# A quarter of the scan steps woven into the attention of the last image, and a sigmoid written as a tanh

## The chip, the core and the metric

The kernel runs on one core of a Trainium2 chip. The core has five engines that run beside each other, each through its own instructions in order: PE (TensorE, matrix products), DVE (VectorE), ACT (ScalarE, activation functions and copies), POOL (GpSimd) and SP (which here only issues DMAs). All data are float32. The metric is the time of one execution in microseconds on the device: 3661.46 us, the median of three runs (3655.79 to 3663.48).

## The reference

Four images of 64 x 64 pixels (L = 4096 tokens) with 128 channels go through four layers one after another:

- layer 0: neighbourhood attention with 7 x 7 windows and a gate, added to x
- layer 1: group norm, then attention of all 4096 tokens to all 4096, added to x
- layer 2: `out = (x W_left + x W_eq) * sum over a row of (x W_right) * sigmoid(x W_gate)`, projected, added to x, layer norm
- layer 3: projection to 512 channels, a 3 x 3 depthwise convolution and SiLU on half of them, then four selective scans, a gate, a norm and an output projection

The scan is what the change is about:

```python
dt_kb = dt.reshape(K, Bb, r, L)              # dt comes as [image, direction]
delta = softplus(delta + dbias); du = delta * u
def step(xc, inp):                           # along the 4096 tokens
    xc = exp(dlt * A) * xc + dut * Bt
    y = xc * Ct
```

The reshapes exchange images and directions in part of the operands: a scan with indices (k, b) takes its delta from image b, and its u, B and C from image k; b and k together say in which of four orders (forward, reversed, transposed, transposed and reversed) they are read. There are 4 k, 4 b and 2 halves f of the 256 channels, so 32 scans of 4096 tokens, 128 channels each. The scans with k and b in {0, 1} need images 0 and 1 only, and no transposed order.

## The kernel before

**Order of the work.** `layers_0_to_2` goes through the images one by one. For each it runs layer 0, then `layer_1`, and woven into `layer_1`'s loop, by the function `between` that is called every eight steps, layer 2 of the same image (`turn`, `mix`, `add`, `norm` by chunks of 512 tokens) and the front of layer 3 (`front`: projection, convolution, SiLU, and the small projection to delta's rank, B and C) of half of the image before and half of this one. What the front makes goes to DRAM: `ub_d` (u times B), `dbl_d` (ten rows: eight for delta, B and C), `ct_d` (C transposed), `zf_d` (the gate) and `y_d` (the sum of the y, which starts as D times u). An odd image adds its part with an accumulating DMA from POOL (line 982), and `copy_du` (line 950) copies that sum to the other three targets. `layer_3` then runs all scans and the output.

A scheduler at compile time orders each engine's instructions by priority (the order of the program) and by its own estimate of when operands are ready; `tc.keep_in_program_order` pins an instruction in its place, and `tc.issue_after(ins)` puts what is traced inside it behind `ins` on that engine.

**`layer_1`** has 16 blocks of 256 queries and 16 groups of 256 keys per block, 279 steps with the run-out. A step multiplies two score tiles (line 636), ACT copies them to SBUF (`st`, 640), DVE keeps a running maximum (`mx`, 642). When a block is complete its maxima are turned (650, 652), spread by a product with ones (`dm`, `pb`, 655 and 659), DVE adds them to the scores (662) and ACT takes the Exp (663), in four pieces of 2048. The values of the block follow 23 steps behind the scores (`po`, 672). PSUM has eight banks: four slots "s" (scores and nearly all 512-column products), two "t", two "o" (`po`). SBUF has five "ring" buffers of 16 KB per partition; in `layer_1` they hold x, the normed x and three rings of scores.

**The end of the last image.** `end(i)` runs the last chunks (4 to 7) of image 3's front, from i = 30 to 40. `diagonals` (line 905, 18 small POOL products) makes the weights with which PE does part of the convolution (`convolve_by_pe`, 918) at i = 35 to 38. At i = 32 the first loads of layer 3 are issued: `early.dbl` (rows of images 0 and 1), `early.ub` and `early.cb` (1085 to 1088).

**`layer_3`** has a list `todo` of 64 pairs of steps of 1024 tokens (128 steps), four k times four parts (f and a pair of b) times four places. A pair takes: two twice-512-column products with eight rows (`pdt`, line 1268), Softplus on ACT (`de`, 1275), `inp = de * ub` on POOL (1279), Exp on ACT into PSUM (`h`, 1292), the scan on DVE (1306), the last column kept (`end`, 1309), the product with C on DVE (`yo`, 1320), and an accumulating DMA from POOL to `y_d` (1321). `load_ub` (1214) and `load_c` (1218) bring u times B and C, four or eight pairs ahead. The k = 0 pairs with b = 0, 1 come first.

Of the kernel before, what the change touches and what calls it, by code (L numbers as in the profile page):

```python
# [29 lines left out]
P = 128  # L30
# [4 lines left out]
CH = 512  # L35
# [46 lines left out]
def conv_seq(ctx, tc, x, mata, matb, cols, rows, rpb, dtw, convw, sel, out):  # L82
# [51 lines left out]
    layers_0_to_2(tc, xf, mata, matb, rows, rpb, convw, sel, ident, cl, dram, big, ring, early, *fronts)  # L134
# [4 lines left out]
def layers_0_to_2(  # L139
    ctx, tc, xf, mata, matb, rows, rpb, convw, sel, ident, cl, dram, big, ring, early, x3_d, ub_d, zf_d, y_d, dbl_d, ct_d, gw_d, bw_d  # L140
# [110 lines left out]
    nc.vector.tensor_scalar(b_rs, cl("b_right"), float(W), None, ALU.mult)  # L251

# [322 lines left out]
    def layer_1(b, xt, hT, st, between):  # L575
# [55 lines left out]
        def score(i, k, g):  # L631
            if g == 0:
                k.mx = tmp.tile([P, G, QB], F32, name="mx1", tag="mx1")
            ps = ps_s([P, G, QB], "sc1")
            for r in range(G):
                nc.tensor.matmul(  # L636
                    ps[:, r, :], lhsT=kT[:, bass.ts(G * g + r, P)], rhs=qT[:, bass.ts(i, QB)], start=True, stop=True
                )
            st = group(ng * i + g)
            nc.scalar.copy(st, ps)  # L640
            if g > 0:
                nc.vector.tensor_tensor(k.mx, group(ng * i) if g == 1 else k.mx, ps, ALU.max)  # L642
# [4 lines left out]
        def turn_maxima(k):  # L647
            pt = ps_t([P, 2, P], "pt1")
            for h in range(2):
                nc.tensor.transpose(pt[:, h, :], k.mx[:, 0, bass.ts(h, P)], ident)  # L650
            nm = sml.tile([P, 2], F32, name="nm1", tag="nm1")
            nc.vector.tensor_reduce(nm, pt, AX.X, ALU.max, negate=True)
            k.dm = tmp.tile([P, 2, P], F32, name="dm1", tag="dm1", bufs=1)
            for h in range(2):
                nc.vector.tensor_scalar(k.dm[:, h, :], ident, nm[:, h:h + 1], None, ALU.mult)

        def soften(i, k):
            pb = ps_t([P, QB], "pb1")
            nc.tensor.matmul(pb, lhsT=ones, rhs=k.dm.rearrange("p h q -> p (h q)"), start=True, stop=True)  # L659
# [22 lines left out]

        blocks = {}
        for s in range(ng * (NB + 1) + LAG):
# [11 lines left out]
            if j >= 0:  # L696
                value(j, blocks[j], gv)
                if gv == ng - 1:
                    finish(j, blocks.pop(j))
            t = s // 8  # L700
# [14 lines left out]
    def layer_2(b, xt):  # L715
# [9 lines left out]
        def mix(n):  # L725
# [4 lines left out]
            nc.vector.tensor_scalar(rt, pr, b_rs, None, ALU.add)  # L730
# [3 lines left out]
            nc.scalar.activation(sg, pg, AF.Sigmoid, bias=cl("b_gate"))  # L734
# [3 lines left out]
            nc.vector.scalar_tensor_tensor(o1, pl, b_le, sg, ALU.add, ALU.mult)  # L738
# [54 lines left out]
    def front(b):  # L793
# [248 lines left out]
        def end(i):  # L1042
# [37 lines left out]
            if i == NT:  # L1080
# [7 lines left out]
                nc.sync.dma_start(early.cb, dbl_d[0][RANK + 1:RANK + 2, :][0].partition_broadcast(P))  # L1088

        def turn(i):  # L1090
# [41 lines left out]
            if b == B - 1 and i == 6:  # L1132
# [4 lines left out]
        return turn  # L1137

# [5 lines left out]
    for b in range(B):  # L1144
# [25 lines left out]
        layer_1(b, xt, *handed.pop(b), between)  # L1170
# [10 lines left out]
def layer_3(ctx, tc, of, dt, na, ident, cl, big, early, x3_d, ub_d, zf_d, y_d, dbl_d, ct_d, gw_d, bw_d):  # L1181
# [34 lines left out]
    def load_c(k, t):  # L1216

        nc.sync.dma_start(cb_s[t], bc_d[k][1 + t][0].partition_broadcast(P))
# [19 lines left out]
    with pool("s", 2) as sp, pool("psC", 2, space=PSUM) as psp:  # L1238
# [5 lines left out]
        for k in range(B):  # L1244
            one, two = k & 1, 1 - (k & 1)
            for part, f in enumerate((one, two, two, one)):
                loads = []
                if part == 0:
                    loads = [(load_ub, two, k), (load_c, k, 1)]
                elif part == 2 and k + 1 < B:  # L1250
                    loads = [(load_c, k + 1, 0)]
                elif part == 3 and k + 1 < B:
                    loads = [(load_ub, two, k + 1)]
                for at_n in range(NSC):
                    n = NSC - 1 - at_n if k & 1 else at_n
                    todo.append((loads, [(f, k, 2 * (part >> 1) + q, n) for q in range(2)]))
# [40 lines left out]
        def back(f, k, b, n, inp, h):  # L1297
# [12 lines left out]
            cb = cb_s[b >> 1]  # L1310
# [247 lines left out]
```

## Time and profile before

| | us |
|---|---|
| median of the runs | 3661.46 |
| profiled execution | 3660.97 |
| its span | 3659.2 |
| PE busy | 3296.5 (90%) |
| DVE busy | 2777.9 (76%) |
| ACT busy | 2645.6 (72%) |
| POOL busy | 1418.6 (39%) |
| layer 1 of the last image, first score to last value | 2413.7 to 2960 |
| scans | 3020 to 3492 |
| output | 3492 to 3659 |

Times inside the span count from its start. In the profile's lists a row has start, duration, engine, line, operation, written tile and read tiles, shapes, count, and in brackets the idle time before it and what ended that. PEld is PE's loading of weights, which runs beside its products. A matmul of float32 has two records. Shares of busy time are means over a window; in the rows by window the numbers behind the five engines are the granted TensorE clock (1 is full), the mean busy share of the 16 DMA engines, and GB/s.

### The profile page before, as it was taken

How to read it: one execution, taken by the hardware profiler on the slowest of the kernel's cores; microseconds unless marked ns; L12 is line 12 of the kernel's file. 1: busy time of each engine (PE TensorE's matmuls, PEld its weight loads, DVE VectorE, ACT ScalarE, POOL GpSimd, SP SyncE). 2: the span in 40 equal slices, each digit the busy share in tenths (PEclk: the TensorE clock that was granted, in tenths of full speed). 3: DMA queues.
4: the chain of work that ended last, by engine and by line, in shares of the span. 5: the costliest groups of instructions: out<-in, count | busy, mean ns of one | idle time of the engine just before them, and what ended most of it. 6: DMA issues, size and time to landing. Idle time of an engine off the chain costs nothing. (4 is left out here: it accounts for less than half of the span.)

```text
span 3659.2 us, 61463 instructions
## 1 busy us (share of the span) xinstructions
PE 3296.5 (90%) x22234; PEld 2603.3 (71%) x22234; DVE 2777.9 (76%) x5069; ACT 2645.6 (72%) x4325; POOL 1418.6 (39%) x1592
## 2 busy tenths in 40 slices
PE   7999999999999999998999999989999987666647
PEld 4679988866788888666888886668888852222236
DVE  5767777767767787676787776767877758999968
ACT  4855667778677777786777777867777769999934
POOL 6500012245112222451122223521222338999856
PEclk8999999999999999999999999999999995555579
DMA  4200000131001012410021213100101279999998
GB/s 125 71 25 3 12 18 27 54 101 34 24 30 41 28 47 86 134 37 24 24 79 30 76 54 101 40 1 24 45 30 36 67 219 217 214 237 218 202 275 282
DMA packets 189362, 310.38 MB, mean 85 GB/s; under 512 B 23007, under 2 KB 111996, under 8 KB 184156
## 3 DMA queue, kind: packets, MB, share of 16 engines
q1 hardware_dynamic: 146260, 220.27, 18.0%
q0 software_dynamic: 24384, 76.95, 11.8%
q10 hardware_dynamic: 18416, 9.24, 0.9%
q8 instruction: 176, 2.88, 0.3%
q14 instruction: 126, 1.03, 0.1%
HBM read 167.69 MB, written 155.56 MB: 88 GB/s over the span
## 5 line engine op out<-in xcount | busy, mean ns | idle before, releaser
L672 PEld LDWEIGHTS po<-v,st 128*128 128x128 f32 x8192 | 1049.1, 193 | 73.6 <-issue 35.7
L672 PE MATMUL po<-v,st 128*128 128x129 f32 x8192 | 1067.9, 277 | 17.6 <-ACT st L663 17.6
L636 PE MATMUL sc<-qT,kT 128*128 128x256 f32 x4096 | 1025.8, 382 | 13.3 <-DVE mx L642 13.1
L640 ACT COPY st<-sc 128x512 f32<-128x512 f32 x1024 | 582.4, 585 | 465.8 <-PE sc L636 463.0
L642 DVE TENSOR_TENSOR mx<-mx,sc 128x512 f32<-128x512 f32 x896 | 613.3, 684 | 283.7 <-ACT st L640 259.4
L636 PEld LDWEIGHTS sc<-qT,kT 128*128 128x128 f32 x4096 | 719.4, 191 | 105.9 <-issue 17.7
L662 DVE TENSOR_TENSOR st<-st,pb 128x2048 f32<-128x2048 f32 x256 | 572.5, 2280 | 29.0 <-PE pb L659 28.7
L663 ACT ACTIVATE st<-st 128x2048 f32<-128x2048 f32 x256 | 484.8, 1911 | 28.8 <-DVE st L662 27.5
L1268 PE MATMUL pdt<-dbl,dt 8*128 8x512 f32 x512 | 307.6, 1081 | 142.1 <-ACT de L1275 141.4
L1279 POOL TENSOR_TENSOR inp<-de,ub 128x1024 f32<-128x1024 f32 x128 | 409.9, 4405 | 9.7 <-ACT de L1275 8.2
L1268 PEld LDWEIGHTS pdt<-dbl,dt 8*128 8x128 f32 x512 | 114.1, 312 | 332.7 <-ACT de L1275 269.8
L503 POOL TENSOR_SCALAR pr<-pr,sm 128x308 f32<-128x308 f32 (+3 forms) x512 | 244.7, 497 | 204.6 <-DVE sm L501 187.6
L743 POOL TENSOR_TENSOR x<-x,row 128x512 f32<-128x512 f32 x32 | 47.9, 1496 | 706.3 <-DVE mx L642 687.6
L889 POOL TENSOR_TENSOR gsum<-gsum,tp 128x504 f32<-128x504 f32 (+1 forms) x177 | 229.7, 1303 | 131.3 <-ACT gsum L877 77.3
L495 ACT ACTIVATE pr<-pr,mx 128x308 f32<-128x308 f32 (+3 forms) x512 | 263.0, 518 | 1.4 <-DVE mx L484 1.4
L1306 DVE TENSOR_TENSOR_SCAN h<-h,end,inp 128x1024 f32<-128x1024 f32 x96 | 221.1, 2346 | 20.0 <-ACT h L1292 9.4
L512 PE MATMUL pt<-ident,pr 128*88 128x128 f32 (+5 forms) x1472 | 205.3, 276 | 9.5 <-ACT prT L514 8.7
L898 DVE SCALAR_TENSOR_TENSOR acc<-xh,cc,acc 128x512 f32<-128x512 f32 (+3 forms) x250 | 198.4, 799 | 16.4 <-ACT acc L862 15.2
L1321 POOL DMA_DIRECT2D y<-yo x112 | 201.7, 2725 | 9.7 <-DVE yo L1320 4.4
L739 POOL TENSOR_TENSOR o<-o,rt 128x512 f32<-128x512 f32 x32 | 34.6, 1082 | 427.9 <-DVE o L738 427.9
L512 PEld LDWEIGHTS pt<-ident,pr 128*88 128x88 f32 (+5 forms) x1472 | 164.5, 138 | 44.7 <-ACT prT L514 25.9
L481 DVE CUSTOM_DVE_ANT_0 pr<-sc,bias_m 128x266 f32<-128x266 f32 (+1 forms) x384 | 152.1, 452 | 55.9 <-PE sc L477 55.2
(234 smaller groups left out, 4993.5 us busy)
## 6 DMA issues: line engine op xcount, KB each, us to landing
y<-yo POOLq DMA_DIRECT2D x112, 512.0 KB, 10.6
y<-y SPq DMA_DIRECT2D x48, 512.0 KB
zf_d<-zf SPq DMA_DIRECT2D x64, 256.0 KB
ub_d<-u SPq DMA_DIRECT2D x64, 256.0 KB
ub<-ub_d SPq DMA_DIRECT2D x16, 1024.0 KB
yl<-y SPq DMA_DIRECT2D x64, 256.0 KB
zc<-zf_d SPq DMA_DIRECT2D x64, 256.0 KB
v_d<-vg SPq DMA_DIRECT2D x128, 64.0 KB
```

The costliest lines, as they stand in the source:

```text
L495: pin(nc.scalar.activation(k.pr[:, h], k.pr[:, h], AF.Exp, bias=k.mx[:, h:h + 1], accum_out=k.sm[:, h:h + 1]))
L503: nc.gpsimd.tensor_scalar(k.pr[:, h], k.pr[:, h], k.sm[:, h:h + 1], 1.0, ALU.mult, ALU.mult)
L512: pin(nc.tensor.transpose(pt[0:n, h, :], k.pr[:, h, at:at + n], ident))
L636: nc.tensor.matmul(ps[:, r, :], lhsT=kT[:, bass.ts(G * g + r, P)], rhs=qT[:, bass.ts(i, QB)], start=True, stop=True)
L640: nc.scalar.copy(st, ps)
L642: nc.vector.tensor_tensor(k.mx, group(ng * i) if g == 1 else k.mx, ps, ALU.max)
L662: nc.vector.tensor_tensor(part, part, pb.unsqueeze(1).to_broadcast([P, 4 * G, QB]), ALU.add)
L663: nc.scalar.activation(part, part, AF.Exp)
L672: nc.tensor.matmul(k.po[:, h, :], lhsT=st[:, r, bass.ts(h, P)], rhs=v[:, j, :], start=(j == 0 and h == 0), stop=(j == NT - 1 and h == 1))
L889: nc.gpsimd.tensor_tensor(a, a, p, ALU.add)
L1268: nc.tensor.matmul(pdt[j][:, g, :], lhsT=dt[o:o + RANK, P * f:P * f + P], rhs=at(dbl[o:o + RANK, :], k & 2, g0, g0 + CH), start=True, stop ...
L1279: nc.gpsimd.tensor_tensor(by_rows(inp), by_rows(de), at(ub_s[f], b ^ (k & 1), SC * n, SC * n + SC), ALU.mult)
```

## The change

1. **Weave.** The 32 steps with k and b in {0, 1} leave `layer_3`. They run as 64 units of 512 tokens inside the last image's `layer_1`, in 16 batches (k, chunk) of four units (f, b), one batch every 15 steps from step 1 on. The units use a fourth ring buffer (the slot of the normed x), a "vg" slot for delta's rows and C, "s" slots for the eight-row products and an "o" slot for the Exp.
2. **`layer_3`** keeps 96 steps (48 pairs), in the order of sides (k, pair of b) below, and other load times. Its first pair now has k = 0 and b = 2, 3.
3. **Layer 2**, in all four images: sigmoid(a) is written as (tanh(a/2) + 1)/2. The half goes into `rt`; the left product's bias is added by an ACT Identity, and DVE's product reads SBUF.
4. **Room.** `diagonals` moves from i = 6 to i = 31; `dm` becomes two tiles of 128 columns, and `pb` two products.

```diff
-            nc.vector.tensor_scalar(rt, pr, b_rs, None, ALU.add)
+            nc.vector.tensor_scalar(rt, pr, b_rs, 0.5, ALU.add, ALU.mult)
...
-            nc.scalar.activation(sg, pg, AF.Sigmoid, bias=cl("b_gate"))
+            nc.scalar.activation(sg, pg, AF.Tanh, bias=b_gh, scale=0.5)
...
-            nc.vector.scalar_tensor_tensor(o1, pl, b_le, sg, ALU.add, ALU.mult)
+            nc.scalar.activation(o1, pl, AF.Identity, bias=b_le)
+            nc.vector.scalar_tensor_tensor(o1, sg, 1.0, o1, ALU.add, ALU.mult)
...
-            if b == B - 1 and i == 6:
+            if b == B - 1 and i == 31:
                 diagonals()
...
-                nc.sync.dma_start(early.cb, dbl_d[0][RANK + 1:RANK + 2, :][0].partition_broadcast(P))
+                nc.sync.dma_start(early.cb, ct_d[0][0].partition_broadcast(P))
...
+            if weave is not None:
+                weave(s, blocks[i].last if i < NB and g > 0 else None)
...
+        def deltas(f, k, n):
+            for b in range(2):
+                ps = ps_s([P, CH], "pdl")
+                nc.tensor.matmul(
+                    ps, lhsT=dt[32 * b:32 * b + RANK, P * f:P * f + P], rhs=dl[32 * b:32 * b + RANK, :],
+                    start=True, stop=True,
+                )
+                nc.scalar.activation(de[f + 2 * b], ps, AF.Softplus, bias=cl("dt_b", 2 * k + f))
...
+        def inputs(j, k, n):
+            nc.gpsimd.tensor_tensor(ub[j % 2], de[j][:, way], ub[j % 2], ALU.mult)
...
+        def decay(j, k, n):
+            a = decays[j] = ps_o([P, CH], "dec")
+            nc.scalar.activation(a, de[j], AF.Exp, scale=na[:, 2 * k + f:2 * k + f + 1])
...
+        def back(j, k, n):
+            nc.vector.tensor_tensor_scan(
+                h[:, way(k ^ b)], a[:, way(k)], ub[j % 2][:, way(k ^ b ^ k)],
+                0.0 if n == first else ends[f, b], ALU.mult, ALU.add,
+            )
+            if n != last:
+                e = ends[f, b] = last_of[:, f, b, n % 2:n % 2 + 1]
+                nc.vector.tensor_copy(e, h[:, 0:1] if k ^ b else h[:, CH - 1:CH])
...
+        def give(j, k, n):
+            nc.gpsimd.tensor_tensor(h, h, cb[:, ::-1] if k else cb, ALU.mult)
+            nc.gpsimd.dma_start(y_d[0][b][f][m // 2][:, CH * (m % 2):CH * (m % 2) + CH], h, accum_op=ALU.add)
...
+        for i, (k, n) in enumerate(batches):
+            s0 = 15 * i + 1
+            at(s0, deltas, 0, k, n)
+            at(s0 + 1, deltas, 1, k, n)
+            if coming:
+                at(s0 + 1, load_dl, *coming)
+            for j in range(4):
+                at(s0 + 2 + 3 * j, inputs, j, k, n)
+                at(s0 + 4 + 3 * j, decay, j, k, n)
+                at(s0 + 5 + 3 * j, back, j, k, n)
+                after = (j + 2, k, n) if j < 2 else (j - 2, *coming) if coming else None
+                if after:
+                    at(s0 + 5 + 3 * j, load_u, *after)
+                at(s0 + 6 + 3 * j, give, j, k, n)
...
-        for k in range(B):
-            one, two = k & 1, 1 - (k & 1)
-            for part, f in enumerate((one, two, two, one)):
+        sides = [(0, 1, (0, 1)), (1, 1, (0, 1)), (2, 0, (0, 1)), (2, 1, (1, 0)), (3, 0, (1, 0)), (3, 1, (0, 1))]
+        for a, (k, t, fs) in enumerate(sides):
+            for p, f in enumerate(fs):
                 loads = []
-                if part == 0:
-                    loads = [(load_ub, two, k), (load_c, k, 1)]
-                elif part == 2 and k + 1 < B:
-                    loads = [(load_c, k + 1, 0)]
-                elif part == 3 and k + 1 < B:
-                    loads = [(load_ub, two, k + 1)]
+                if a == 0 and p == 0:
+                    loads = [(load_ub, 1, 0), (load_c, 1, 1, 1)]
+                elif a == 0:
+                    loads = [(load_ub, 0, 1)]
+                elif a == 1 and p == 0:
+                    loads = [(load_c, 2, 0, 0), (load_ub, 1, 1)]
+                elif a == 1:
+                    loads = [(load_ub, 0, 2)]
+                elif a == 2 and p == 0:
+                    loads = [(load_c, 2, 1, 1), (load_ub, 1, 2)]
+                elif a == 3 and p == 0:
+                    loads = [(load_c, 3, 0, 0)]
+                elif a == 3:
+                    loads = [(load_ub, 1, 3)]
+                elif a == 4 and p == 0:
+                    loads = [(load_c, 3, 1, 1), (load_ub, 0, 3)]
```

`load_dl` loads delta's rows of both images for a chunk, `load_u` a unit's u times B (256 KB), `load_cs` C for one b spread over the partitions (256 KB); all three issue on SP. `weave(s, last)` runs what is planned for step s; a `back` is put behind the step's maximum on DVE.

## The prediction

> **What bounds the kernel now.** I read the busy time by stage first, because the page's averages mix stages with different limits. The columns are: window, its length, then busy time and count for PE, PEld, DVE, ACT and POOL, then the granted TensorE clock, the DMA share and GB/s.
>
> ```profile
> 2414.00:2960.00 546.00, 533.28 (x3486) 469.68 (x3484) 425.19 (x615) 406.41 (x537) 145.83 (x136) 0.99 0.14 44
> 2960.00:3020.00 60.00, 49.38 (x218) 25.13 (x219) 28.59 (x50) 27.74 (x46) 22.70 (x21) 0.89 0.87 246
> 3020.00:3262.00 242.00, 167.44 (x287) 63.08 (x286) 222.60 (x179) 229.45 (x202) 226.92 (x133) 0.50 0.98 218
> ```
>
> The first row is layer 1 of the last image: PE is busy 533.3 of 546 us, so a matmul added there lengthens it by its whole duration. ACT is at 74%, DVE at 78%, POOL at 27%. The third row is the scans with k = 0 and 1: DVE, ACT and POOL are all above 90% and DMA at 0.98. The change takes work from the third row and puts it into the first.
>
> Second view: the timeline of DVE in the scans, cut to each part's first scans (4 pairs make a part).
>
> ```profile
> 3027.53 4.52 DVE L1306 TENSOR_TENSOR_SCAN h<-h,inp 128x1024 f32<-128x1024 f32 x2 [5.36 <-ACT h L1292]
> 3060.61 4.48 DVE L1306 TENSOR_TENSOR_SCAN h<-h,inp 128x1024 f32<-128x1024 f32 x2 [0.19 <-ACT h L1292]
> 3088.66 4.48 DVE L1306 TENSOR_TENSOR_SCAN h<-h,inp 128x1024 f32<-128x1024 f32 x2 [0.19 <-ACT h L1292]
> ...
> 3261.76 2.30 DVE L1306 TENSOR_TENSOR_SCAN h<-h,inp 128x1024 f32<-128x1024 f32 x1 [0.19 <-ACT h L1292]
> ```
>
> k = 2 begins at 3261.76, so the 32 pairs of k = 0 and 1 take 3261.76 - 3027.53 = 234.2 us. An undisturbed part takes 3088.66 - 3060.61 = 28.05, 7.01 a pair; the first took 33.1, 5 over, and one more (3144.76 to 3177.54) 4.7 over, with DVE waiting for a `y<-yo` store behind loads.
>
> **What the scan stage saves.** 16 of these 32 pairs go; k = 2 and 3 stay. 16 x 7.01 = 112.2 us remain. Two things are added.
>
> First, the start. Today the first 8 pairs (56 us) use images 0 and 1, loaded early. Afterwards the first pair needs image 3's `dbl`. SP's timeline:
>
> ```profile
> 3019.50 1.41 SPq L967 DMA_DIRECT2D dbl_d<-dq  x4
> 3022.60 5.66 SPq L950 DMA_DIRECT2D y<-y  x7
> 3028.30 0.52 SPq L1231 DMA_DIRECT2D dbl<-dbl_d  x1
> 3028.94 1.98 SPq L1214 DMA_DIRECT2D ub<-ub_d  x2
> ```
>
> That load is issued at 3028.30, behind seven 512 KB copies (7.3 MB read and written; near 300 GB/s, about 24 us). Today's first `pdt` is at 3020.61. The load can't be in before some 3031, and was in by 3054.36, when POOL reads the `ub` issued after it. So the start slips by 10 to 34 us; I take 23, from the copies' bytes. The first stores go to `y_d[0][2]` and `[0][3]`, which those copies read and write: the same wait. Behind it on POOL stand the next `inp` products, on ACT and DVE nothing that could start.
>
> Second, loads. For k = 0 and 1 both `ub` halves are now used for 8 pairs, not 16: 12 MB in 16 pairs, where today it is 8. Two overruns of 5 us per 32 pairs become, by bytes per pair, about 15 us in all (10 to 30). New time of this part: 112.2 + 15 + 23 = 150; **saving 84 us** (102 to 57 with the bounds).
>
> **What layer 1 pays.** PE: 64 matmuls of 8 rows by 512 columns. The row is the same operation at the start of the scans, beside a full 128x512 product (x counts two records per matmul):
>
> ```profile
> 2947.11 1.88 PE L848 MATMUL pz<-x3k,win 128*128 128x512 f32 x4
> 3020.61 2.24 PE L1268 MATMUL pdt<-dbl,dt 8*128 8x512 f32 x8
> ```
>
> Four `pdt` take 2.24 us, 0.56 each, two full products 1.88, 0.94 each: two `pdt` at different partitions run beside each other. The new ones come in twos at partitions 0 and 32, so 64 x 0.56 = **36 us**; issued apart, 64 x 0.94 = 60.
>
> ACT: 64 Softplus and 64 Exp of 512. The nearest row is L734, 128x512 with a column operand, 687 ns: 128 x 0.687 = 88 us. Eight Identity of layer 2 add 5.5. Then the table loads, seen in ACT's timeline of the scans:
>
> ```profile
> 3079.11 1.28 ACT L1292 ACT_TABLE_LOAD   x1
> 3080.41 2.28 ACT L1292 ACTIVATE h<-de,na 128x1024 f32<-128x1024 f32 x2
> 3082.71 1.28 ACT L1275 ACT_TABLE_LOAD   x1
> 3084.00 2.12 ACT L1275 ACTIVATE de<-pdt,col 128x1024 f32<-128x1024 f32 x2
> ```
>
> Softplus and Exp need one load each at every change. Each of 16 batches has Softplus in two consecutive steps: 32 loads if both steps share one and one Exp load follows, 64 if not, 128 if every Softplus stands alone. I take 48, 61 us. Tanh isn't in the trace; I leave its loads as Sigmoid's (L734: 32 loads), between that and none. ACT: 406.4 + 88 + 5.5 + 61 = 561 us in a stage of 546 + 36 = 582: 96%.
>
> In this trace a load costs 1.28 us and the next ACTIVATE starts 0.01 later. The Trainium skill (ScalarE: Activation LUTs, What ACT_TABLE_LOAD costs) puts a switch at 2.66 us, with a drain of 1.38 behind the load; no drain shows here. By it the 48 loads would be 128 us, ACT 628, the stage +82 and the sum 3663, no measurable change. The same page (Table sets) has tanh in the set of exp, which would take 8 loads, 10 us, off ACT here; no run has shown that yet.
>
> DVE: 64 scans of half of L1306's 2.346 us, 75 us, and 56 copies of 0.149, 8: 425.2 + 83 = 508, 87%. Layer 2's product stays one DVE instruction. POOL: 128 products of about 1.3 us (L739 1.08, L743 1.50) and 64 DMA issues near 1.1 (`y<-du`): 146 + 236 = 382, 66%. DMA: 64 accumulating stores of 256 KB at half of 3.33 us (two of 512 KB per 7.01 us fill 0.95 of the engines where they run alone), 107 us, and 25 MB of loads at 300 GB/s, 83: share 0.14 to 0.46. None of these is a bound.
>
> But PE, ACT and DVE then stand at 100, 96 and 87%, all in order, and the new waits couple them. `pdl` holds two of the four "s" slots until a Softplus has read it; scores and values queue behind on PE. The Exp waits for an "o" slot that `po` also uses; behind it stand the `st` copies that free score slots. `back` waits for POOL's product, which waits for an SP load, which waits for the `back` two units before; behind `back` are maxima and the additions ahead of softmax, behind the POOL product the `gsum` additions that free ACT's `tp` buffers, behind the SP load the loads of the next convolution chunk. Today PE loses about 13 us in this stage with ACT and DVE in the seventies. I take 20 us of new stalls; bounds 0 (the steps left between each pair of operations hide all) and 60 (a wait of 2 us, as today's longest `pb` wait of 2.5, in each of 32 Softplus steps).
>
> Sum of layer 1: 36 + 20 = 56 (36 to 120).
>
> **Small edits.** `diagonals` moves from i = 6 to 31: 18 POOL operations of 0.68, 12 us, into 2925 to 2965, where POOL is busy some 20 of 40 us. Its reader, the convolution on PE, comes later; +4 (0 to 12). The tanh form in images 0 to 2 takes nothing from PE and moves ACT by less than 10 us an image beside 26% idle: 0 (-10 to +10; cover gone, ACT's own time). `dm` in two halves: two 128-column matmuls for one of 256, 0.
>
> **Sum**, on the profiled execution (3660.97 us, span 3659.2 and 1.8 around it; median of the runs 3661.46, the same within 0.02%): 3660.97 - 84 + 56 + 4 = **3637 us**.
>
> **Rivals.** (a) The weave hides: no stalls, start 10 us late, overruns 10. -102 + 36: 3595. For it: 546 us with 15 steps per batch of 4 units. Against: ACT at 96%.
>
> (b) Nearly all is given back: stalls 40 and the rest as forecast, 3657; no measurable change. For it: four score slots cut to two while ACT is in a burst (2602 to 2618 it has no gap of 0.5 us). Against: one deltas step in eight steps of layer 1.
>
> (c) Slower: ACT becomes layer 1's bound, through table loads, if nearly every Softplus stands alone between Exp work. 128 loads are 164 us, ACT 406 + 88 + 5.5 + 164 = 664, stage +118: 3660.97 - 84 + 118 + 4 = 3699. It decides from ACT = 546 + 80 = 626, about 98 loads. For it: Copy, Exp and Silu already alternate here. Against: the two Softplus of one step follow each other.
>
> **How the numbers follow.** About 0.2% (7.3 us) is what a measurement can tell from no change. Forecast, 3612 to 3653: 0.50; (a) with all below 3612: 0.15; (b), 3654 to 3669: 0.13; (c) and all above: 0.22. Faster 0.65, same 0.13, slower 0.22. The range leaves out the lower third of (a) and the upper part of (c): 3598 to 3694.
>
> **What would show it.** Scans after layer 1 about 84 us shorter, with 96 scans of 1024; the first `pdt` 10 to 34 us after the last `dbl_d<-dq`; layer 1 near 600 us with PE still above 92%; added table loads between 32 and 64. Wrong if ACT shows 100 or more, if PE waits on `pdl` or `sc` for over 40 us in sum, or if the first scan stage's parts run well over 28 us each.

## The result, and the profile after

The changed kernel takes 3742.88 us (median of four runs, 3741.76 to 3744.33) where the kernel before takes 3662.47 beside it: a ratio of 1.0221, 95% interval 1.0208 to 1.0234. It is slower by 80 us; the forecast was 24 us faster. The profiled execution took 3743.82 us with a span of 3742.0, so the spans differ by 82.8 us. Stage by stage, with the start of a stage taken from its first instruction in each trace:

| | before | after | forecast | measured |
|---|---|---|---|---|
| to the first score of the last image (tanh form in images 0 to 2) | 2413.7 | 2406.8 | 0 | -6.9 |
| layer 1 of the last image | 545.3 | 734.1 | +56 | +188.8 |
| from there to the first `pdt` | 61.6 | 59.9 | +4 | -1.7 |
| scans, first `pdt` to last scan | 470.5 | 379.8 | -84 | -90.7 |
| output | 168.1 | 161.4 | 0 | -6.7 |

One stage is off. (The -6.9 of the first row is no more than runs with the same work ahead of that point differ by, as told below.) The stage rows of the changed kernel (columns as in the prediction; the first is layer 1 of the last image, the third the scans with k = 0 and 1):

```profile
2407.00:3141.00 734.00, 646.96 (x3639) 520.91 (x3638) 550.93 (x732) 561.86 (x728) 367.66 (x328) 0.91 0.38 90
3141.00:3201.00 60.00, 49.51 (x231) 25.94 (x230) 29.59 (x53) 27.65 (x47) 23.51 (x22) 0.91 0.90 256
3201.00:3344.00 143.00, 92.61 (x151) 34.30 (x151) 111.79 (x90) 117.56 (x103) 120.10 (x67) 0.51 0.89 212
```

In the first row no engine is full: PE is busy 88% of the stage, ACT 77%, DVE 75%, POOL 50%, and the granted clock is 0.91 where it was 0.99. The sums of ACT, POOL and DMA came out near their forecast (ACT 561 and 561.9; POOL 382 and 368; DMA share 0.38); the stage they stand in is 133 us longer than the 601 that was forecast (545.3 + 56). From rows of one microsecond each over the stage, the PE time that is idle (one minus its busy share) is 87.0 us, and was 12.7; the time lost to a granted clock below 1 (one minus the clock) is 63.1 us, and was 3.4. Where the clock falls it falls to 0.50, called half clock here. So 74 us of the 188.8 are waits of PE, 60 are half clock, and the other 55 are, by subtraction, what the 64 products add to PE's busy time at full clock.

PE's waits in that stage (columns: who waits for whom, us in total, times, longest), the first four of the changed kernel:

```profile
PE pb L662 <- DVE dm L657: 25.9, 15, 5.6
PE sc L638 <- DVE mx L644: 23.8, 12, 3.7
PE pt L297 <- DVE st L665: 10.6, 4, 4.3
PE pdl L1177 <- ACT scans L1181: 5.0, 2, 3.7
```

and the first two of the kernel before:

```profile
PE pb L659 <- DVE dm L655: 5.0, 3, 2.5
PE po L672 <- ACT st L663: 4.8, 1, 4.8
```

The wait for which the prediction had a mechanism, a product or score behind a Softplus, is the smallest of the four. PE waits for DVE: for the short `dm` that it multiplies into `pb`, for the short maximum that frees a score slot, and, in the middle of a turned block `pt`, for the end of DVE's additions ahead of the softmax. One such place, DVE's timeline first:

```profile
2793.20 1.92 DVE L657 TENSOR_SCALAR dm<-ident,nm 128x128 f32<-128x128 f32 x2
2795.04 3.51 DVE L775 TENSOR_SCALAR x<-x,mv,rd 128x128 f32<-128x128 f32 x2
...
2802.62 6.67 DVE L665 TENSOR_TENSOR st<-st,pb 128x2048 f32<-128x2048 f32 x3
```

and PE's in the same stretch:

```profile
2804.68 0.49 PE L297 MATMUL pt<-ident,x 128*128 128x128 f32 x3
2809.44 0.66 PE L297 MATMUL pt<-ident,x 128*128 128x128 f32 x2 [4.27 <-DVE st L665]
2809.95 2.08 PE L638 MATMUL sc<-qT,kT 128*128 128x256 f32 x4
...
2822.01 1.18 PE L1177 MATMUL pdl<-dlc,dt 8*128 8x512 f32 x4
2823.13 1.13 PE L638 MATMUL sc<-qT,kT 128*128 128x256 f32 x4
```

Two `dm` take 1.92 us and two normed pieces of x 3.51 (one `dm` was 392 ns on average before); three additions of 2.28 us each (given as one row of 6.67) follow without a gap, with a maximum still behind them, and PE stands for 4.27 us until the last of them ends. Then the clock falls: four records of scores take 2.08 us, and 1.13 again at 2823. The clock in windows of one to two microseconds (behind the five busy times):

```profile
2807.00:2808.00 1.00, 0.00 (x0) 0.00 (x0) 1.00 (x2) 0.87 (x1) 0.00 (x0) 1.00 0.00 0
2809.00:2810.00 1.00, 0.56 (x3) 0.35 (x3) 1.00 (x3) 1.00 (x3) 0.00 (x0) 0.50 0.00 0
2820.00:2822.00 2.00, 2.00 (x9) 1.70 (x8) 0.69 (x1) 1.53 (x2) 0.23 (x1) 0.50 0.95 148
2824.00:2826.00 2.00, 2.00 (x16) 1.87 (x15) 0.00 (x0) 1.99 (x4) 0.87 (x1) 1.00 0.11 18
```

So a wait of 4.3 us costs about 11 us: a stretch of 13.7 us at half clock begins near its end, 6.8 lost. There are 20 stretches at half clock in this stage, and one in the kernel before.

The rest of the change did what was forecast. The scans of the changed kernel, first of a part:

```profile
3226.67 4.48 DVE L1434 TENSOR_TENSOR_SCAN h<-h,inp 128x1024 f32<-128x1024 f32 x2 [24.43 <-ACT h L1420]
...
3259.75 4.48 DVE L1434 TENSOR_TENSOR_SCAN h<-h,inp 128x1024 f32<-128x1024 f32 x2 [0.18 <-ACT h L1420]
...
3344.35 4.48 DVE L1434 TENSOR_TENSOR_SCAN h<-h,inp 128x1024 f32<-128x1024 f32 x2
```

The first scan is 25.9 us behind the first `pdt` (6.9 before): a slip of 19, forecast 23. What is waited for is the load of `dbl`, as forecast:

```profile
3219.21 3.78 PE L1396 MATMUL pdt<-dbl,dt 8*128 8x512 f32 x4 [11.90 <-DMA dbl<-dbl_d]
```

The 16 pairs take 3344.35 - 3226.67 = 117.7 us, 5.5 over 16 times 7.01 (forecast 15).

The table loads of layer 1 (ACT's groups; count, then busy us and mean ns):

```profile
L1181 ACT ACT_TABLE_LOAD x30 | 38.5, 1283 | 7.0 <-PE pdl L1177 6.5
L1191 ACT ACT_TABLE_LOAD x29 | 37.2, 1283 | 5.1 <-DVE scans L1202 4.7
...
L741 ACT ACT_TABLE_LOAD x1 | 1.3, 1283 | 0.0
```

The weave has 59, between the bounds of 32 and 64 and near the 48 that were taken. Tanh has one load in all of the kernel, where Sigmoid had 32.

### The profile page after: what moved, and what is told of

It is laid out like the page before. It is cut to its first block, busy times and chain, and to the rows that moved or that the text cites. A ratio compares the mean times of both kernels' runs of the same rounds, so it can differ in the third digit from the quotient of the medians.

```text
span 3742.0 us, 62196 instructions
## 1 busy us (share of the span) xinstructions
PE 3333.9 (89%) x22362; PEld 2628.3 (70%) x22362; DVE 2787.2 (74%) x5102; ACT 2671.3 (71%) x4420; POOL 1535.3 (41%) x1720
## 4 chain that ended last, share of the span: by engine, by line
PE 57%; DVE 14%; issue 9%; ACT 9%; POOL 6%; DMA 5%; SPq 0%; ACTq 0%; DVEq 0%; POOLq 0%
PE po L675 17%; PE sc L638 16%; PE pt L514 4%; DVE st L665 3%; PE sc L479 3%; PE po L525 2%; POOL inp L1407 2%; DVE mx L644 2%; DVE acc L906 2%; POOL y L1449 2%; ACT st L666 1%; PE pp L535 1%; PE pz L856 1%; DMA yl<-y 1%; DVE h L1434 1%
## 5 line engine op out<-in xcount | busy, mean ns | idle before, releaser
L675 PEld LDWEIGHTS po<-v,st 128*128 128x128 f32 x8192 | 1063.9, 196 | 78.3 <-issue 40.2
L675 PE MATMUL po<-v,st 128*128 128x129 f32 x8192 | 1086.6, 279 | 12.9 <-ACT st L666 12.8
L638 PE MATMUL sc<-qT,kT 128*128 128x256 f32 x4096 | 1049.8, 388 | 40.2 <-DVE mx L644 34.6
L638 PEld LDWEIGHTS sc<-qT,kT 128*128 128x128 f32 x4096 | 727.7, 194 | 160.2 <-DVE mx L644 40.8
L665 DVE TENSOR_TENSOR st<-st,pb 128x2048 f32<-128x2048 f32 x256 | 572.6, 2280 | 23.9 <-PE pb L662 23.9
L1396 PE MATMUL pdt<-dbl,dt 8*128 8x512 f32 x384 | 236.9, 1079 | 122.1 <-ACT de L1403 107.6
L1407 POOL TENSOR_TENSOR inp<-de,ub 128x1024 f32<-128x1024 f32 x96 | 323.4, 5313 | 27.1 <-DMA gw<-gw_d 17.4
L1396 PEld LDWEIGHTS pdt<-dbl,dt 8*128 8x128 f32 x384 | 86.7, 311 | 269.5 <-ACT de L1403 203.4
L906 DVE SCALAR_TENSOR_TENSOR acc<-xh,cc,acc 128x512 f32<-128x512 f32 (+3 forms) x250 | 225.5, 913 | 10.0 <-ACT acc L870 8.3
L514 PEld LDWEIGHTS pt<-ident,pr 128*88 128x88 f32 (+5 forms) x1472 | 165.0, 139 | 45.4 <-ACT prT L516 25.9
L1449 POOL DMA_DIRECT2D y<-yo x80 | 186.8, 3814 | 6.1 <-DVE yo L1448 2.6
L516 ACT COPY prT<-pt 110x512 f32<-110x512 f32 (+3 forms) x240 | 139.0, 579 | 69.7 <-PE pt L514 69.3
```

The lines of the kernel that those rows point to most:

```text
L514: pin(nc.tensor.transpose(pt[0:n, h, :], k.pr[:, h, at:at + n], ident))
L638: nc.tensor.matmul(ps[:, r, :], lhsT=kT[:, bass.ts(G * g + r, P)], rhs=qT[:, bass.ts(i, QB)], start=True, stop=True)
L665: nc.vector.tensor_tensor(part, part, pb.unsqueeze(1).to_broadcast([P, 4 * G, QB]), ALU.add)
L675: nc.tensor.matmul(k.po[:, h, :], lhsT=st[:, r, bass.ts(h, P)], rhs=v[:, j, :], start=(j == 0 and h == 0), stop=(j == NT - 1 and h == 1))
L906: nc.vector.scalar_tensor_tensor(acc, x, c, acc, ALU.mult, ALU.add)
L1396: nc.tensor.matmul(pdt[j][:, g, :], lhsT=dt[o:o + RANK, P * f:P * f + P], rhs=at(dbl[o:o + RANK, :], k & 2, g0, g0 + CH), start=True, stop ...
```

## The experiments

**The theories.** The expectations name them by letters, and some letters change their meaning. A (all runs): PE bounds the stage, so its new work is paid in full, and what is added to DVE is paid almost in full too, because DVE's short steps (`dm`, the maxima) come late, PE waits, and each wait is followed by half clock; that POOL slows DVE is part of it in e1. B (e1 to e4): ScalarE's table loads and bursts set the pace. C: the PSUM slots that wait for Softplus and Exp (e1 to e7), and in e12 ScalarE as the bound, by its table loads. D: in e1 to e4 PE's own products and what they displace; in e9 that DVE's idle time has room for the scans and the loss lies elsewhere. E (e11): the place of the units in a block of layer 1.

All were profiled once beside a run of the kernel before on the same chip (3658.6 to 3666.3 us), except the one marked. "Layer 1" is that of the last image; "idle" and "half clock" are PE's, from rows of 1 us as above. The first score, ahead of which all variants of the changed kernel do the same, lies between 2404.7 and 2411.9 us, so stage lengths are good to a few us. e1 to e4, e9, e10 and e12 to e15 leave out part of the computation, so their totals are not those of a usable kernel.

| run | what is in | total | layer 1 | over 545.3 | idle | half clock |
|---|---|---|---|---|---|---|
| before | no weave | 3661 | 545.3 | | 13 | 3 |
| e12 | activations alone | 3590.0 | 580.2 | 35 | 35 | 7 |
| e9 | scans alone | 3601.7 | 590.9 | 46 | 44 | 12 |
| e10 | products alone | 3620.0 | 602.2 | 57 | 14 | 14 |
| e13 | products, activations | 3642.5 | 630.7 | 85 | 26 | 20 |
| e14 | products, scans | 3647.6 | 635.5 | 90 | 35 | 22 |
| e15 | all three, unchained | 3674.6 | 660.2 | 115 | 42 | 24 |
| e2 | all but the scans | 3660.9 | 652.2 | 107 | 38 | 29 |
| e4 | all but the products | 3687.5 | 680.2 | 135 | 97 | 53 |
| e1 | all but POOL's products | 3722.1 | 711.8 | 167 | 81 | 61 |
| e3 | all, 56 table loads fewer | 3728.0 | 713.4 | 168 | 79 | 56 |
| e7 | all, products in "t" slots | 3733.1 | 714.5 | 169 | 68 | 50 |
| e6 | all, Exp in place | 3738.2 | 726.4 | 181 | 78 | 61 |
| after | all | 3742.9 | 734.1 | 189 | 87 | 63 |
| e11 | all, period 16 | 3777.4 | 755.8 | 210 | 96 | 72 |
| e8 | all, crowded places | 3782.1 | 772.1 | 227 | 121 | 68 |

### One part away from the whole: e1, e2, e3, e4

```diff
e1
-            nc.gpsimd.tensor_tensor(ub[j % 2], de[j][:, way], ub[j % 2], ALU.mult)
...
-            nc.gpsimd.tensor_tensor(h, h, cb[:, ::-1] if k else cb, ALU.mult)
```

> The changed kernel with both POOL products of every unit left out (delta times u, and the state times C; the scan reads u as loaded, the state is stored as it is). Layer 1 of the last image takes 734 us in the changed kernel and 546 in the one before. Theory A, DVE is late and POOL makes it later: DVE's operations that read SBUF return to their old durations (acc 1.28 to about 0.85 us, dm 0.78 to about 0.40), DVE's busy time falls by about 40 us, layer 1 shrinks by 50 to 90 us, total 3655 to 3695. Theory B, ACT's table loads and bursts set the pace: less than 20 us, 3725 to 3745. Theory C, the PSUM slots: less than 20 us. Theory D, PE's own products (55 us) and what they displace: less than 20 us.

Measured: layer 1 22 us shorter, less than the 50 to 90 of A, a little more than the 20 of the others. POOL's products do slow DVE (without them DVE is busy 518.5 us instead of 550.9). But e1 has a stall of its own that the changed kernel does not have. Without POOL's second product nothing reads `cb`, and SP issues 21 loads of it in a row (under `dlc`, the name of its slot), ahead of the first loads of u. SP, then DVE:

```profile
2365.38 64.73 SPq L1170 DMA_DIRECT2D dlc<-dbl_d  x21
2430.20 0.85 SPq L1167 DMA_DIRECT2D scans<-ub_d  x2
```

```profile
2434.39 1.22 DVE L1201 TENSOR_TENSOR_SCAN scans<-dec,scans 128x512 f32<-128x512 f32 x1 [14.54 <-DMA scans<-ub_d]
```

The changed kernel issues its first loads of u at 2369.51. By the starts of the scores, e1 is 35 us behind the kernel before when the third of the 16 blocks begins, the changed kernel 14 and e15 8. From there to the last value e1 loses another 132 us, the changed kernel 175. So POOL's products cost about 43 us where the stall does not hide it, and are no small part of the loss.

```diff
e2
-            nc.vector.tensor_tensor_scan(
-                h[:, way(k ^ b)], a[:, way(k)], ub[j % 2][:, way(k ^ b ^ k)],
-                0.0 if n == first else ends[f, b], ALU.mult, ALU.add,
-            )
...
-                nc.vector.tensor_copy(e, h[:, 0:1] if k ^ b else h[:, CH - 1:CH])
```

> The changed kernel without the scans and their end columns on DVE inside layer 1 (POOL's second product reads delta instead of the state). Theory A: DVE loses about 85 us of work, layer 1 shrinks by 80 to 130 us, total 3615 to 3665. Theory B and D: less than 30 us, 3715 or more. Theory C: an o slot is now free as soon as the Exp has written it, so 10 to 40 us.

Measured: 82 us shorter, for 85 us of DVE time (550.9 to 465.6); half clock falls from 63 to 29 us, idle from 87 to 38. The biggest single part, as A expected (80 to 130), though DVE was idle a quarter of the stage. With the scans go also the waits of other engines for them (ACT's Exp, below), so the 82 us are not the price of DVE's time alone; e9 has that.

```diff
e3
-                nc.scalar.activation(de[f + 2 * b], ps, AF.Softplus, bias=cl("dt_b", 2 * k + f))
+                nc.scalar.activation(de[f + 2 * b], ps, AF.Exp, bias=cl("dt_b", 2 * k + f))
```

> The changed kernel with Exp in the place of Softplus inside layer 1, so that no table changes between the two (other numbers come out). Theory A: ACT loses the 59 added table loads, 75 us of busy time, but layer 1 shrinks by less than 30 us, total 3715 or more. Theory B: it shrinks by 60 us or more, 3685 or less. Theory C: the slots are held 1.3 us less for every second Softplus, 10 to 30 us. Theory D: less than 10 us.

Measured: lines 1181 and 1191 have 11 loads instead of 59, line 666 has 5 instead of 12, line 741 none instead of one: 56 fewer, 72 us at 1.283. ACT's busy time falls by 72 us, the stage by 21 only, which fits A (under 30) and the slots of C (10 to 30), and not B. Table loads are not what bounds it.

```diff
e4
-                nc.tensor.matmul(
-                    ps, lhsT=dt[32 * b:32 * b + RANK, P * f:P * f + P], rhs=dl[32 * b:32 * b + RANK, :],
-                    start=True, stop=True,
-                )
-                nc.scalar.activation(de[f + 2 * b], ps, AF.Softplus, bias=cl("dt_b", 2 * k + f))
+                nc.scalar.activation(de[f + 2 * b], win, AF.Softplus, bias=cl("dt_b", 2 * k + f))
```

> The changed kernel without the 64 eight-row products inside layer 1; Softplus reads another tile that lies in SBUF, so PE's work and the two s slots are not used. Theory A: only PE's own 55 us go, and a little of the clock, total 3675 to 3695. Theory C: 55 us and the waits on the slots, layer 1 shrinks by 100 us or more, 3645 or less. Theory D: the whole loss but the scans that ACT and DVE still do, 100 us or more, as in C; PE's waits on DVE remain in neither. Theory B: 40 to 60 us.

Measured: 54 us shorter, about what the products add to PE's own time, and in the range of A (and of B, 40 to 60). PE's idle time even rises to 97, so the waits do not need the "s" slots that the products hold. The edit is not clean, though: Softplus and Exp alternate more often in it (88 loads on their two lines instead of 59), and ACT is busy 36 us longer.

### The small edit alone: e5

The kernel before with point 3 of the change and nothing else (ten runs against thirteen of the kernel before):

```diff
-            nc.scalar.activation(sg, pg, AF.Sigmoid, bias=cl("b_gate"))
+            nc.scalar.activation(sg, pg, AF.Tanh, bias=b_gh, scale=0.5)
...
-            nc.vector.scalar_tensor_tensor(o1, pl, b_le, sg, ALU.add, ALU.mult)
+            nc.scalar.activation(o1, pl, AF.Identity, bias=b_le)
+            nc.vector.scalar_tensor_tensor(o1, sg, 1.0, o1, ALU.add, ALU.mult)
```

> The kernel before with the tanh form of layer 2 alone, no weave. In the changed kernel the last image's layer 1 starts 7 us earlier (2406.8 against 2413.7), and the first three layer 1 stages are 2 to 3 us shorter each. If the tanh form does that, this kernel takes 3651 to 3657, faster by 0.1 to 0.3%. If the split of dm or another order of the instructions did it, the time stays at 3660 to 3665.

Measured: 3657.68 us against 3662.36, a ratio of 0.9988 (0.9978 to 0.9997). That is just above the 3651 to 3657 expected of the tanh form. It leaves nothing out and is below both kernels, by an amount at the edge of what can be measured.

### Links of the chain, and places in the block: e6, e7, e8, e11

In e6 the Exp writes over its input instead of an "o" slot; in e7 the products use the "t" slots:

```diff
e6
-            a = decays[j] = ps_o([P, CH], "dec")
+            a = decays[j] = de[j]
e7
-                ps = ps_s([P, CH], "pdl")
+                ps = ps_t([P, CH], "pdl")
```

> The changed kernel with the Exp of the weave written over delta in SBUF and not into a PSUM slot that the values use too. Theory C (slots): ACT no longer waits for the scan of the unit before (26 us of waits in layer 1), layer 1 falls from 734 us by 25 or more, total 3718 or less. Theory A (DVE late): the scans read more from SBUF beside POOL and stay as many, change within 15 us, 3728 to 3758.

> The changed kernel with the eight-row products in the two t slots and not in the four s slots of the scores. Theory C: scores keep four slots, layer 1 falls by 20 us or more, 3723 or less. Theory A: within 15 us, or longer, since pb and the turned maxima use the t slots, 3730 to 3765.

Measured: 8 and 20 us shorter in layer 1 (5 and 10 in the total). e6 does not remove a link, it changes one for another: the Exp now writes over the delta that POOL's product has yet to read. ACT's waits for the scans (32.2 us, below) are gone, and it waits for POOL instead:

```profile
ACT scans L1191 <- POOL scans L1186: 67.3, 30, 6.0
```

So what the "o" slot alone costs is not shown by e6. In e7 PE's waits for the maxima at `sc` fall from 23.8 to 1.2 us, and most of this comes back as other waits (idle 68 instead of 87): the slots cost something, and are not the loss.

```diff
e8 (with e6's edit)
-            s0 = 15 * i + 1
+            s0 = 16 * i + 8
...
-                at(s0 + 5 + 3 * j, back, j, k, n)
+                at(s0 + (3, 4, 7, 8)[j], back, j, k, n)
e11
-            s0 = 15 * i + 1
+            s0 = 16 * i + 6
...
-                at(s0 + 5 + 3 * j, back, j, k, n)
+                at(s0 + (5, 8, 11, 14)[j], back, j, k, n)
```

> As e6, and one batch per block of 16 steps at a fixed place: deltas at steps 8 and 9, scans at 11, 12, 15 and 16 of the block, away from steps 2 to 8, where DVE adds the maxima and ACT takes the Exp. If DVE is late because scans fall between the additions of 2.28 us, layer 1 falls against e6 by 40 us or more (total 3700 or less). If only the amount of DVE's work counts (85 us, one for one, as e2 showed it), the change is under 20 us. If crowding four units into six steps makes ACT or POOL the late one, it grows.

> The whole weave, whose batch of four units repeats every 16 steps of layer 1 instead of every 15 (a block of layer 1 has 16 steps), so that each scan meets the same place of each block; shifted by six steps, and the units three steps apart as before, with no crowding. Nothing is left out. Theory A (the total of the work added to VectorE and TensorE counts, and the late steps are spread over all places): layer 1 of the last image stays within 20 us of the 734 us of the changed kernel. Theory E (the weave loses because its units drift through the block and meet the statistics of the softmax at bad places): layer 1 is under 705 us, or over 760 if this place is the bad one.

Measured: 38 us longer than the changed kernel (46 than e6) when the four units are crowded into half a block, 22 longer when each meets a fixed place three steps apart. e11 is 2 us outside the 20 that A allowed and below the 760 of E. The units' place matters, but neither fixed place helped, and the drifting one of the change is the best of the three.

### Parts alone: e9, e10, e12, and together: e13, e14, e15

These leave the other parts out by not planning them; e10 and e14 also drop the Softplus that follows each product, e12 the products. Where scans stand without their Exp they read a standing tile:

```diff
e9, e14, e15
-            h, a = hs[j % 2], decays.pop(j)
+            h, a = hs[j % 2], win
...
-                h[:, way(k ^ b)], a[:, way(k)], ub[j % 2][:, way(k ^ b ^ k)],
+                h[:, way(k ^ b)], a[:, way(k)], win[:, way(k ^ b ^ k)],
```

> One part alone, from the side of the kernel before: of the weave only the 64 scans of VectorE are left in layer 1 of the last image, and the 48 small copies of their ends; their operands are one standing tile that no other work writes, so that they wait for nothing. No products on TensorE, no Softplus and Exp, no GpSimd work and no transfers of the weave are left, so images 0 and 1 get no scan term from steps 0 and 1 and the output is not the reference's. Layer 1 of the last image took 545 us without the weave and 734 with it. VectorE has 22% of that stage idle (some 120 us by the busy times), the scans are 77 us of busy time. Theory A (VectorE's work is charged to the path about one for one even where VectorE is idle a fifth of the time, because TensorE waits in turn for short VectorE steps that then come late, and each wait is followed by a stretch of half clock): layer 1 is 615 to 650 us, TensorE's idle time rises to 35 to 60 us and the clock loss to 20 to 40. Theory D (VectorE's idle time takes them up, and only all parts together make the loss): layer 1 is under 575 us.

> The other part alone: of the weave only the 64 products of the deltas on TensorE are left, with the loads of their rows; Softplus, the GpSimd products, Exp, the scans, the give-back and its transfers are left out, so the output is not the reference's. A lone 128x512 product takes 0.56 us in the place it was moved from. Theory A (TensorE pays its own work, and no more): layer 1 of the last image is 585 to 605 us (545 and 40 to 60), the clock loss stays under 10 us. If the half clock is not a consequence of waits but of the products themselves, the loss is over 20 us here too. If the products lie in idle time of TensorE, layer 1 stays under 565.

Measured: scans alone 46 us for 94 of DVE time: between the two theories, half is hidden and half is paid, mostly in PE's idle time (44 instead of 13), with half clock at 12, under the 20 to 40 of A. Products alone 57 us with PE idle no more than before: as A had it, but with 14 us of half clock, not under 10. Some 10 of the 57 us are therefore half clock, and some 46 the products' own time.

> Of the weave only ScalarE's 64 Softplus and 64 Exp are left, with the table loads that they bring; Softplus reads a standing tile instead of a product. No products, scans, GpSimd work or transfers of the weave, so the output is not the reference's. Layer 1 of the last image was 545 us without the weave, 734 with it, 591 with the scans alone, 602 with the products alone. Rival C (ScalarE becomes what bounds: table loads in the way of the copies of the running maximum): layer 1 is over 600 us here. Theory A (ScalarE has the room, its work alone is nearly free): 545 to 570 us, TensorE idle under 30.

> The products on TensorE with the Softplus and Exp that follow them, as in the changed kernel; no scans, no GpSimd work, none of the transfers but the loads of the products' rows; the output is not the reference's. If costs add: the products alone cost 57 us, so layer 1 is 602 us and what the activations alone cost. If the crossing of two streams is charged extra: over 20 us above that sum; the run without scans, which has GpSimd's products and all transfers besides, took 652.

> The scans on VectorE (on a standing tile) and the products on TensorE; no Softplus, Exp, GpSimd work or transfers but the loads of the products' rows; the output is not the reference's. If costs add: 545 + 46 + 57 = 648 us. If the crossing of the two streams is charged extra (VectorE later, TensorE's waits longer, more half clock): 670 to 710 us, with TensorE's idle time over 60.

Measured: activations alone 35 us, between C's 600 and A's 570, with ACT busy 94% of the stage; PE's idle time is 35, not under A's 30. Pairs do not cost more than their sum: 85 for 57 + 35, and 90 for 57 + 46. The extra charge for the crossing of two streams, which A had come to, falls.

> Products on TensorE, Softplus and Exp on ScalarE and the scans on VectorE together, but the scans read a standing tile instead of Exp's result and the inputs; no GpSimd products, no transfers but the loads of the products' rows; the output is not the reference's. If costs only add: 545 + 86 + 46 = 677 us for layer 1 of the last image, or somewhat less, as scans and products together cost less than their sum. If the three streams in one stage are charged extra by crossing alone: over 700 us (the run without GpSimd's products, which has the chain and the transfers, took 712). Under 690 the rest is the chain and the transfers.

Stage rows of e15 and, below, of the run without POOL's products (e1):

```profile
2408.00:3068.00 660.00, 617.88 (x3639) 499.58 (x3638) 520.92 (x732) 556.25 (x726) 155.65 (x136) 0.96 0.12 37
```

```profile
2405.00:3117.00 712.00, 630.65 (x3643) 511.94 (x3642) 518.50 (x732) 561.74 (x728) 197.85 (x200) 0.91 0.36 87
```

DVE and ACT do the same amount of work in both (521 and 519, 556 and 562 us). In e15 no scan waits for an Exp or a load, no Exp for a scan, and the u, B, C and y transfers are gone: 115 us over the kernel before. With them (e1) it is 167, with twice the idle time of PE and 61 us of half clock instead of 24. So 52 us come from the chain between the streams and its transfers, with the stall at e1's start among them; from the third block on, where that stall is over, it is 132 to 107 us, 24. What the chain does on DVE and ACT, in the changed kernel's waits of that stage, DVE's and ACT's:

```profile
DVE scans L1202 <- DMA y<-scans: 10.4, 8, 2.7
```

```profile
ACT dec L1191 <- DVE scans L1202: 32.2, 19, 6.3
```

Both engines work in order: while a scan waits for the give-back DMA that still reads its buffer, the maxima stand behind it, and while an Exp waits for a scan, the `st` copies do. Which share belongs to the transfers and which to each wait was not separated.

**What the runs settle.** Layer 1's 188.8 us, added in this order: products 57; scans on top of them 33; activations on top of both 25 (e15: 115); chain and transfers 52 (e1: 167); POOL's products 22. Another order gives the parts other shares, and the last two are distorted by e1's start: from the third block on they are 24 and 43. The plain work of the three streams, 115 us, is already more than the 90.7 that the scan stage gives back; e15, without chain and POOL's part, is still no faster than the kernel before beside it (3674.6 and 3666.3, one run each).

## Why the prediction was wrong, step by step

- **What bounds the kernel.** PE bounds layer 1: right, and e10 confirms it. The reading that ACT at 74% and DVE at 78% leave room was the weak half: e9 and e12 show that a stream alone on such an engine costs the stage a half or a quarter of its busy time (46 of 94, 35 of 138).
- **Scan stage, 84 us saved:** right; 90.7 measured from the first `pdt` to the last scan. Slip 19 for 23, overruns 5.5 for 15.
- **PE, 64 x 0.56 = 36 us:** too small. Products cost 45 to 57 us (e9 to e14 45, e12 to e13 50, e4 54, e10 57 with 10 of half clock), 0.7 to 0.9 each. A pair side by side does take 1.13 us, 0.56 each. But by the starts of their records only 19 of the 32 pairs ran so in the changed kernel; the other products ran one after another, at about 1.1 each (0.94 in the prediction).
- **"I take 20 us of new stalls; bounds 0 … and 60": the step that failed.** The term was 134 us: 74 of PE's waits and 60 of half clock. Two things were wrong. The waits were placed at the Softplus and the `pdl` slots, where 9.5 us of waits lie (5.0 before `pdl`, 4.5 before scores); most lies at `pb`, `sc` and `pt`, behind DVE. And a wait was priced at its length, while with most of the longer ones comes a stretch at half clock, which begins in the gap or within 3.5 us behind it: at 18 of the 22 gaps above 1.5 us and none of the 17 between 0.3 and 1 us (of those that began at full clock). In sum the half clock cost nearly as much again. That DVE's work is what makes PE wait is shown by e2 (idle 38 without the scans) and e9 (44 with the scans alone).
- **ACT 561 us, 48 loads:** right in size (561.9 us, 59 loads). DVE 508: 43 too low, mostly since its own operations were stretched beside POOL (e1 takes 32 of it away). POOL and DMA right.
- **Sum of layer 1:** 56 forecast, 189 measured; 19 of the difference are the products and 114 the stalls.
- **Diagonals +4, tanh 0:** the stage behind layer 1 changed by -1.7 us; the tanh form alone took -4.7 us (e5).
- **Rivals.** (c) had the direction and the nearest number (3699), by another mechanism: it needed 98 loads and ACT full, and ACT was 77% busy with 59. That its loads cost little is shown by e3 (72 us of loads away, 21 us back). (a) and (b) fall with the stalls.
- **The marks.** Layer 1 near 600 us with PE above 92% would have shown the error (734, 88%). "Over 40 us on `pdl` or `sc`" did not: the two sum to 39.4 of 87 us idle. The mark watched the wrong waits. The mark on the first `pdt` (10 to 34 us after the last `dbl_d<-dq`) missed too: it came 1.1 us after. The wait for `dbl` stood at a later product, as shown above.
- **The Trainium skill** (ScalarE: Activation LUTs, What ACT_TABLE_LOAD costs) puts a drain of 1.38 us on top of each load of 1.28; on which side of the load it does not say. In the changed trace a load at 2813.41 starts 0.02 us behind the copy before it, ends at 2814.69, and the next ACTIVATE starts at 2814.70; e3's 56 fewer loads lower ACT's busy time by 72 us, 1.28 each. No drain shows on either side. The same page (Table sets) was right on tanh: one load where Sigmoid had 32.

## What to carry to other kernels

In a stage bound by one engine, a "free" quarter of another engine is free only for work that can wait: if the bounding engine waits in turn for short steps on that other engine, added work there cost a quarter to a half of its length here, and nearly all of it for the scans once they were chained to other engines. Where the clock was near full before, price a new wait of TensorE of 2 us or more at up to twice its length; waits under 1 us had no such stretch behind them here. Before weaving, add up what the three streams cost the bounding stage without any chain; if this is already more than the other stage gives back, the chain can only add to it, and the two other placings tried here added more still. And look at what else an edit moves before reading its difference: leaving out one part reordered the loads in e1 and doubled a wait in e6.

## What the runs showed of the hardware

**Half clock after short gaps.** In the kernel before, layer 1 lost 3.4 us to the clock; the changed one lost 63.1 in 20 stretches of about 3.4, 7, 10 or 14 us, 18 of them after PE had been idle for 1.3 to 5.6 us. The Trainium skill (TensorE: Matmul & The Clock Gate, What's actually happening) says that the clock is set by windows of some 3.4 us, low after an idle one and high after a busy one; the lengths fit this. Gaps of 1.7 to 2.2 us were enough for five of the 20, shorter than the window that the page names.

**Half clock without a gap.** In e10 two of the five stretches begin with PE busy all the time, just behind products of eight rows:

```profile
2635.25 1.12 PE L1177 MATMUL pdl<-dlc,dt 8*128 8x512 f32 x2
2636.30 1.30 PE L638 MATMUL sc<-qT,kT 128*128 128x256 f32 x4
2637.40 1.50 PE L675 MATMUL po<-v,st 128*128 128x129 f32 x6
2638.82 2.08 PE L1177 MATMUL pdl<-dlc,dt 8*128 8x512 f32 x4
2640.83 2.08 PE L638 MATMUL sc<-qT,kT 128*128 128x256 f32 x4
```

The granted clock is 0.56 from 2637 and 0.50 from 2638 to 2643. It is no chance. Over layer 1 of the last image in all traces, 32 stretches begin with less than 0.5 us of idle PE in the 6.8 us before. In each of the 32 there are products of eight rows in those 6.8 us, though the time just behind such products is only about 0.3 of the stage. The five runs without these products (before, e4, e5, e9, e12) have 29 stretches in it, and none that begins so. That such narrow products count little as activity would explain it; what it is about them is not shown.

**POOL stretches DVE.** DVE's `acc` (line 906), which reads two SBUF tiles, took 804 ns on average before, 1200 in the changed kernel and 845 without POOL's products; `dm` took 392, 717 and 542. Groups of `acc` in layer 1 of the kernel before, of the changed one and of e1:

```profile
L898 DVE SCALAR_TENSOR_TENSOR acc<-xh,cc,acc 128x504 f32<-128x504 f32 (+2 forms) x72 | 57.4, 804 | 2.7 <-ACT acc L862 2.5
```

```profile
L906 DVE SCALAR_TENSOR_TENSOR acc<-xh,cc,acc 128x504 f32<-128x504 f32 (+3 forms) x72 | 84.4, 1200 | 0.4
```

```profile
L906 DVE SCALAR_TENSOR_TENSOR acc<-xh,cc,acc 128x504 f32<-128x504 f32 (+3 forms) x72 | 58.8, 845 | 1.6 <-ACT acc L870 1.1
```

In e8, with POOL working back to back, one `acc` took 7.67 us. The additions (line 665, 2280 ns before and 2279 after) and the maxima of the scores (684 and 679), which read one operand from PSUM, did not change. POOL's woven products are not all of it: the fold of the maxima (line 647, two SBUF tiles) took 422 ns before, 848 in the changed kernel, and 1082 without them.
